# A perceiver block planned anew: measured overlaps, waits for buffers at first use, and one context buffer per batch

## The chip, the cores and the metric

The kernel runs on one core of a Trainium2 chip. The metric is the device time of one execution in microseconds (us), and 0.2% of it is 3.3 us. Five engines work side by side: TensorE (PE, with its weight loads as PEld), VectorE (DVE), ScalarE (ACT), GpSimd (POOL) and SyncE (SP), which only issues transfers. Each works through its own list of instructions in order, and waits for the others where data or buffers require it.

## The reference

One block with two layers on 32 batches of 64 latents, width 256, with 256 context rows per batch, all in float32. What the change touches is the first part, the cross attention, and the order of everything:

```
kv_in  = concat(norm(ctx)[256 rows], norm(x)[64 rows])   # per batch: 320 rows
q      = norm(x) Wq ;  k = kv_in Wk ;  v = kv_in Wv      # 16 heads of 64
x      = x + softmax(q k^T / 8) v Wo                     # cross attention
x      = x + linear_attention(norm(x))
x      = x + ffn(norm(x))                                # int weights, dequantised
x      = x + attention(norm(x), norm(ctx)), masked
x      = x + slstm(norm(x))
x      = x + experts(norm(x))        # routed by an entmax over the experts
```

## The kernel before

**Tiles and stages.** The 2048 latent rows are 16 tiles of 128 rows, so a tile t holds the batches 2t and 2t+1. The kernel has three stages. The first is the cross attention over 32 batches, about 0 to 854 us. The second runs linear attention, feed forward, attention, sLSTM and router in 8 groups of two tiles, to about 1390 us. The third runs the experts on gathered rows, to the end.

**The cross attention.** For a pair of batches, `l0_context` loads two contexts into one tile `cx` of 128x1024 (four row tiles of 256), norms the four row tiles, and applies gain and offset (`affine`) on GpSimd in instructions over the whole tile. Two such tiles fit (`ar.put(1, "cx", ...)`). `l0_keys` transposes a batch's context (`tr_c`) into `cT`. `l0_scores` has eight score matmul groups (`sc`, two heads each; first the four with even numbers, then the odd ones). Each has a maximum on DVE (`nmax`) and an exp on ACT, which also sums. After four of them come a reciprocal, a divide of 128x1280 on DVE and three stream transposes. When both halves are there, sixteen pieces are moved into `pT`: four on GpSimd, four on ACT or DVE, eight as transfers from SP. `l0_applied` multiplies with the normed context (`pu`): twice, two pairs of matmuls with 128 rows, and one pair with 64 rows for the latents' part. Each result is copied to `uT` on ACT or DVE. `l0_projected` projects a pair of batches: `po`, which reads the copies, and then `pw`. For every four batches `l0_queries` makes norms, transposes, `pq` and the eight products `pqk`, whose copies fill the buffers `qk`.

**Second and third stage.** Names beginning with `la` (`lakv`, `lakvs`, `lac`, `laq`) belong to linear attention, `ff` to feed forward, `xa`, `xsc`, `xpTp`, `xpo`, `xpw` to attention, `sl` to sLSTM, `me`, `lg` and `gT_ps` to the router, and `mepha`, `mepya`, `mephb`, `mepyb`, `rl`, `rg`, `tr_xg` to the experts. Names that begin with `tr_` are transpositions on TensorE.

**The order.** No instruction's place is written out by hand. The kernel first lists all operations with their operands and a rank (`pl.rank`), and then a planner (`Plan.run`) replays a model of the chip. Among the operations whose predecessors are placed and whose buffers have room, it takes the one that can start first, and among equals the one with the lower rank; it looks at most a fixed number of ranks ahead. It issues that operation at once, so the order in which it picks is the order of each engine's list. The planned times themselves are not kept: on the chip only data, buffers and the order count. The model has a length for each instruction (`PlanEngine.length`), one for each TensorE group (`together(length)`), and 0.06 us (`HOP`) from the end of one instruction to a dependent one on another engine. `copy` and `either` are operations that ACT or DVE can do; the planner chooses the engine that can start sooner. A tile takes a place in `Slots` or in an `Area` when its first operation is issued; the place comes free after the last one that uses it. Every instruction is recorded by the one line in `issue`, which is why all rows of the profile show L375. The core of the planner's choice:

```python
for engine, (length, _) in op.ways.items():
    at = free[engine]
    for other in op.before:
        at = max(at, other.end if other.on == engine and other.end == other.done else other.done + self.HOP)
    for t_ in op.uses:
        at = max(at, t_.free_at)
    key = at, op.rank
    if best is None or key < best[0]:
        best = key, op, engine
...
op.end = op.done = free[engine] = at + length
```

Of the kernel before, what the change touches and what calls it, by code (L numbers as in the profile page):

```python
# [8 lines left out]
F32 = mybir.dt.float32  # L9
# [5 lines left out]
P = 128  # L15
# [139 lines left out]
class Slots:  # L155
# [5 lines left out]
    def room(self, t_, k):  # L161
        return len(self.free) > k and (not self.in_order or self.asked[self.next + k] is t_)

    def take(self, t_):
        self.free.sort()
        self.next += 1
        return self.free.pop(0)
# [5 lines left out]
class Area:  # L173
# [9 lines left out]
    def room(self, t_, k):  # L183
        i = (self.next + k) % len(self.places)
        if k >= len(self.places) or self.asked[self.next + k] is not t_ or self.live[i] is not None:
            return False
        return all(a.next == len(a.asked) and a.live[j] is None for a, j in self.rivals[i])

    def take(self, t_):
        i = self.next % len(self.places)  # L190
# [19 lines left out]
class Plan:  # L210
# [8 lines left out]

    ENGINES = {"PE": "tensor", "DVE": "vector", "ACT": "scalar", "POOL": "gpsimd", "SP": "sync"}  # L220
    HOP = 0.06

    def __init__(self, tc):
        self.tc, self.ops, self.slots, self.news = tc, [], {}, []
# [25 lines left out]
    @contextmanager  # L250
    def together(self, length):

        assert self.group is None
        self.group = []
        yield
        calls, self.group = self.group, None
        self.add({"PE": (length, calls)})

    def add(self, ways):
        op = Op()  # L260
# [38 lines left out]
    def run(self, ahead):  # L299
        free = dict.fromkeys(self.ENGINES, 0.0)  # L300
        busy = dict.fromkeys(self.ENGINES, 0.0)
        wire = 0.0
        ready = [op for op in self.ops if op.left == 0]
        todo = len(self.ops)
        waiting = set(self.ops)
        rest = sorted(self.ops, key=lambda op: -op.rank)
        while todo:
            best, short = None, None
            while rest[-1] not in waiting:
                rest.pop()  # L310
            for op in sorted(ready, key=lambda op: op.rank):
                if short is not None and op.rank > short.rank and "PE" in op.ways and op.news:
                    continue
                if op.rank > rest[-1].rank + ahead:
                    continue
                at = 0.0
                if op.news and not self.has_room(op):
                    if "PE" in op.ways and (short is None or op.rank < short.rank) and self.has_room(op, True):
                        short = op
                    continue  # L320
                for engine, (length, _) in op.ways.items():
                    at = free[engine]
                    for other in op.before:
                        at = max(at, other.end if other.on == engine and other.end == other.done else other.done + self.HOP)
                    for t_ in op.uses:
                        at = max(at, t_.free_at)
                    key = at, op.rank
                    if best is None or key < best[0]:
                        best = key, op, engine
            assert best is not None, "nothing can start"  # L330
            (at, _), op, engine = best
            length, calls = op.ways[engine]
            todo -= 1
            ready.remove(op)
            waiting.remove(op)
            op.on = engine
            op.end = op.done = free[engine] = at + length
            busy[engine] += length
            if "dma" in calls[0][0]:
                size = PlanEngine.size_of(calls[0])  # L340
                wire = max(wire, op.end) + size / 380e3
                op.done = max(wire, op.end + size / 220e3) + (2.4 if engine == "POOL" else 1.5)
            self.issue(op, engine, calls)
            for other in op.after:
                other.left -= 1
                if other.left == 0:
                    ready.append(other)
        self.now, self.busy = max(op.done for op in self.ops), busy

    def has_room(self, op, later=False):  # L350

        taken = {}
        for t_ in op.news:
            s_ = t_.slots
            if later and not s_.in_order:
                continue
            k = taken.get(id(s_), 0)
            if not s_.room(t_, k):
                return False
            taken[id(s_)] = k + 1  # L360
        return True

    def issue(self, op, engine, calls):
        for t_ in op.news:
# [74 lines left out]
class PlanEngine:  # L439
# [33 lines left out]
    @staticmethod  # L473
    def length(engine, name, args, kw):

        if "dma" in name:
            return (0.65 if isinstance(kw["in_"], View) and isinstance(kw["out"], View) else 0.4) if "indirect" not in name else 1.55 if "compute_op" in kw else 1.25
        o = args[0] if args else kw["out"]
        n = 1
        for a in [o] + [a for a in args[1:] if isinstance(a, View)]:  # L480
            m = 1
            for k in a.shape[1:]:
                m *= k
            n = max(n, m)
        if name == "memset":
            return 0.1 + 0.5e-3 * n
        if engine == "ACT":
            if isinstance(kw.get("scale"), View):
                return 0.6
            return (0.12 + 0.91e-3 * n if name == "copy" else 0.33 + 0.66e-3 * n) + (0.19 if "accum_out" in kw else 0)  # L490
        if engine == "DVE":
            return 0.15 + 1.04e-3 * n + (0.08 if name == "tensor_tensor_reduce" else 0)
        if engine == "POOL":
            return 0.7 if n < 64 else 0.3 + 2.0e-3 * n
        return 0.18 if name == "transpose" else max(0.36, 1.67e-3 * n)


# [1 line left out]
def kernel(ctx: ExitStack, tc: tile.TileContext, d: dict, out: bass.AP):  # L499
# [130 lines left out]
    with ExitStack() as sa:  # L630
# [18 lines left out]
        ar.put(1, "gb", 1024, 10240)  # L649
        for n, tag in enumerate(("la", "ls", "latT")):  # L650
            ar.put(1, tag, 512, 11264 + 512 * n, 12800 + 512 * n)
        ar.put(1, "cx", 1024, 14336, 15360)
        ar.put(1, "cT", 640, 16384, 17024)
        ar.put(0, "gbcol", 256, 17664, 17920)
        ar.put(1, "qk", 1024, *range(17664, 25856, 1024))
# [118 lines left out]
        def l0_context(t):  # L774

            pl.rank = 2 * t - 6.0
            cx = ar.tile([P, 4, D], F32, tag="cx", name=f"cx{t}")
            for b2 in range(2):
                b = 2 * t + b2
                pl.sync.dma_start(  # L780
                    out=cx[:, 2 * b2 : 2 * b2 + 2, :],
                    in_=d["ctx"][b * S2 : (b + 1) * S2, :].rearrange("(t p) d -> p t d", p=P),
                )
            if t == 0:
                load_w(wv, "l0x_wkv", slice(1024, 2048))
                load_w(wo, "l0x_wo")
            if t == 2:

                nxt["a_wq"] = ar.tile([P, KD, D], F32, tag="a_wq", name="a_wq")
                pl.sync.dma_start(out=nxt["a_wq"], in_=d["a_wq"].rearrange("(k p) n -> p k n", p=P))  # L790
                nxt["a_wkv"] = ar.tile([P, KD, 2 * D], F32, tag="a_wkv", name="a_wkv")
                pl.sync.dma_start(out=nxt["a_wkv"], in_=d["a_wkv"].rearrange("(k p) n -> p k n", p=P))
                nxt["rows_a"] = ar.tile([P, 4 * D], F32, tag="rows_a", name="rows_a")
                pl.sync.dma_start(out=nxt["rows_a"], in_=d["rows"][:, 0 : 4 * D].to_broadcast([P, 4 * D]))
                pl.sync.dma_start(out=rows, in_=d["rows"][:, 4 * D :].to_broadcast([P, NROWS - 4 * D]))
            pl.rank = 2 * t - 3.0
            srcs = [cx[:, i, :] for i in range(4)]
            norm(srcs, srcs, f"c{t}", "c")
            affine(cx, 0, 4)
            return cx  # L800

        def l0_queries(g):
# [52 lines left out]
        def l0_keys(b, lt, cx):  # L855

            pl.rank, pl.lane = b - 1.2, "k"
            b2, b4 = b % 2, b % G
            cT = ar.tile([P, KD, SK], F32, tag="cT", name=f"cT{b}")
            pst = bank([P, KD, S2], f"tr_c{b}")  # L860
            with pl.together(T4):
                for kd in range(KD):
                    for i in range(2):
                        tr(pst[:, kd, i * P : (i + 1) * P], cx[:, 2 * b2 + i, kd * P : (kd + 1) * P], ident)
            pl.gpsimd.tensor_copy(cT[:, :, S2:SK], lt[:, :, b4 * S : (b4 + 1) * S])
            pl.copy(cT[:, :, 0:S2], pst)
            return cT
# [58 lines left out]
        def l0_applied(b, pT, cx, la, ls, uT):  # L926
# [5 lines left out]
            for kd in range(KD):  # L932
                f_ = slice(kd * P, (kd + 1) * P)
                pus = [bank([P, 4, 4, 32], f"pu{b}_{kd}_{jj}") for jj in range(2)]
                for jj in range(2):
                    with pl.together(1.75):
                        for n in range(2):
                            rhs = pT[:, 2 * n + jj].rearrange("p a j c -> p j a c")
                            mm(pus[jj], cx[:, 2 * b2 + n, f_], rhs, start=(n == 0), stop=False)
                with pl.together(1.04):  # L940
                    for jj in range(2):
                        h_ = slice(64 * jj, 64 * jj + 64)
# [991 lines left out]
```

## Time and profile before

| What | us |
|---|---|
| median of 3 runs (lowest, highest) | 1634.33 (1632.51, 1634.55) |
| profiled execution | 1633.02 |
| its span, first to last instruction | 1631.3 |
| first and last matmul in the span | 5.3, 1617.5 |

Of the costliest groups, some rows (engine, operation, tiles and shapes, count, then busy us and mean ns of one):

```profile
L375 PE MATMUL pu<-arena 128*128 128x512 f32 (+1 forms) x768 | 301.0, 615 | 3.5 <-ACT arena L375 2.8
L375 PE MATMUL sc<-arena 128*128 128x320 f32 x1024 | 290.5, 436 | 0.0
L375 ACT ACTIVATE arena<-sc,nmax 128x320 f32<-128x320 f32 x256 | 134.4, 527 | 250.3 <-DVE nmax L375 241.8
L375 DVE TENSOR_TENSOR arena<-arena,sm 128x1280 f32<-128x1280 f32 x64 | 108.1, 1690 | 2.2
```

The column after the last bar is the idle time of the engine just before these instructions, and what ended it. ACT waits long for DVE's maxima, but idle time of an engine that isn't the bottleneck costs nothing: TensorE's rows show next to none. On GpSimd by shape, the affine of the contexts and the same work in the second stage:

```profile
L375 POOL TENSOR_TENSOR arena<-arena 128x1024 f32<-128x1024 f32 x32 | 80.8, 2526 | 43.5 <-ACT arena L375 40.6 <-PE sc L375 1.7
...
L375 POOL TENSOR_TENSOR arena<-arena 128x512 f32<-128x512 f32 x16 | 21.6, 1351 | 22.4 <-DVE arena L375 12.1 <-ACT arena L375 9.6
```

### The profile page before, as it was taken

The numbers are of one execution on the slowest core, as the hardware profiler recorded it, in microseconds if no ns is written. First come the engines' busy times: TensorE is split into PE (matmuls) and PEld (weight loads), VectorE is DVE, ScalarE is ACT, GpSimd is POOL, SyncE is SP. The second block draws the span as 40 slices with busy tenths as digits, with TensorE's granted clock in tenths as the row PEclk, the third lists the DMA queues.
The fourth block names the chain that finished last, engine by engine and source line by source line (L and its number), as shares of the span: only waits on it lengthen the run. The fifth ranks groups of instructions, "written<-read, shape, count | busy, mean of one in ns | idle before, by whom it ended". The sixth has DMA issues, their size and how long they took to land. (4 is left out here: it accounts for less than half of the span.)

```text
span 1631.3 us, 25951 instructions
## 1 busy us (share of the span) xinstructions
PE 1579.4 (97%) x9226; PEld 1106.8 (68%) x9226; DVE 1088.2 (67%) x3089; ACT 693.8 (43%) x1813; POOL 422.1 (26%) x524
## 2 busy tenths in 40 slices
PE   8999999999999999999989999999999999999996
PEld 6556656565665656666556777777777776878885
DVE  6657666676766757776755788888888788762230
ACT  4434344353533535334421454454544547432332
POOL 5123123230333223331311221221212112223342
PEclk9999999999999999999999999999999999999998
DMA  6112112121112211122121000010000220455391
GB/s 212 38 30 59 38 31 44 38 59 29 39 30 46 47 34 40 30 71 53 38 54 49 14 27 27 18 37 14 27 27 20 85 80 19 133 144 141 69 307 31
DMA packets 95601, 95.02 MB, mean 58 GB/s; under 512 B 9327, under 2 KB 85936, under 8 KB 95472
## 3 DMA queue, kind: packets, MB, share of 16 engines
q1 hardware_dynamic: 89952, 85.41, 19.2%
q0 software_dynamic: 5520, 7.94, 2.4%
q8 instruction: 74, 1.21, 0.3%
q14 instruction: 55, 0.45, 0.1%
HBM read 63.63 MB, written 7.47 MB: 44 GB/s over the span
## 5 line engine op out<-in xcount | busy, mean ns | idle before, releaser
L375 PE MATMUL pu<-arena 128*128 128x512 f32 (+1 forms) x768 | 301.0, 615 | 3.5 <-ACT arena L375 2.8
L375 PE MATMUL sc<-arena 128*128 128x320 f32 x1024 | 290.5, 436 | 0.0
L375 PEld LDWEIGHTS sc<-arena 128*128 128x128 f32 x1024 | 190.8, 190 | 95.3 <-issue 19.2
L375 ACT ACTIVATE arena<-sc,nmax 128x320 f32<-128x320 f32 x256 | 134.4, 527 | 250.3 <-DVE nmax L375 241.8
L375 PEld LDWEIGHTS pu<-arena 128*128 128x128 f32 (+1 forms) x768 | 113.9, 189 | 175.9 <-issue 159.1
L375 POOL COPY arena<-arena 32x640 f32<-32x640 f32 (+1 forms) x161 | 108.9, 676 | 404.1 <-DVE arena L375 300.4
L375 DVE TENSOR_REDUCE nmax<-sc 128x1 f32<-128x320 f32 x256 | 121.8, 484 | 105.5 <-PE sc L375 104.1
L375 POOL TENSOR_TENSOR arena<-arena 128x1024 f32<-128x1024 f32 (+3 forms) x72 | 118.5, 1646 | 166.6 <-DVE arena L375 109.7
L375 ACT ACTIVATE arena<-arena,xnm 128x256 f32<-128x256 f32 x256 | 127.1, 500 | 52.1 <-DVE xnm L375 51.9
L375 DVE COPY arena<-pu 128x512 f32<-128x512 f32 x62 | 42.7, 689 | 115.4 <-PE pu L375 115.2
L375 DVE CUSTOM_DVE_ANT_0 arena<-xsc,arena 128x256 f32<-128x256 f32 x256 | 101.2, 421 | 17.7 <-ACT arena L375 10.3
L375 DVE TENSOR_TENSOR arena<-arena,sm 128x1280 f32<-128x1280 f32 x64 | 108.1, 1690 | 2.2
L375 DVE STREAM_TRANSPOSE arena<-arena 128x512 f32<-128x512 f32 (+1 forms) x192 | 104.4, 594 | 3.6
L375 ACT COPY arena<-pu 128x512 f32<-128x512 f32 x66 | 38.4, 585 | 128.0 <-PE pu L375 128.0
L375 POOL DMA_INDIRECT out<-arena x25 | 39.6, 1585 | 102.8 <-DVE arena L375 71.2
L375 PE MATMUL pqk<-arena 64*128 64x256 f32 x512 | 63.1, 383 | 1.6 <-ACT arena L375 1.6
L375 PE MATMUL xpTp<-ident,arena 128*128 128x128 f32 x512 | 63.6, 274 | 0.9 <-ACT arena L375 0.9
L375 PE MATMUL xak<-arena 128*128 128x512 f32 x128 | 62.3, 610 | 0.0
L375 PEld LDWEIGHTS xpTp<-ident,arena 128*128 128x128 f32 x512 | 56.9, 141 | 7.2 <-DVE arena L375 2.2
L375 PE MATMUL xav<-arena 128*128 128x256 f32 x256 | 61.5, 384 | 0.0
L375 PEld LDWEIGHTS po<-arena 128*64 128x64 f32 x1024 | 55.5, 137 | 8.8 <-issue 8.3
L375 PE MATMUL mepha<-arena 128*128 128x256 f32 x256 | 60.1, 385 | 1.4 <-ACT arena L375 1.4
(395 smaller groups left out, 2800.9 us busy)
## 6 DMA issues: line engine op xcount, KB each, us to landing
arena<-in_m_w SPq DMA_DIRECT2D x26, 1024.0 KB
arena<-arena SPq DMA_DIRECT2D x256, 80.0 KB
arena<-in_ctx SPq DMA_DIRECT2D x32, 256.0 KB
arena<-in_ctxT SPq DMA_DIRECT2D x16, 512.0 KB
x<-in_x SPq DMA_DIRECT2D x16, 128.0 KB
arena<-in_l0x_wkv SPq DMA_DIRECT2D x2, 1024.0 KB
arena<-arena SPq DMA_DIRECT2D x16, 128.0 KB
out<-x SPq DMA_DIRECT2D x16, 128.0 KB
```

The lines of the kernel that those rows point to most:

```text
L375: r = getattr(real, name)(*[get(a) for a in args], **{k: get(a) for k, a in kw.items()})
```

## The change

The planner's model gets five corrections, and one tile is cut in two.

- After an instruction, DVE is free for the next 0.085 us before its end, ACT 0.11, POOL 0.05.
- An operation that depends on one of the same engine can start 0.03 us after that one's end instead of at its end.
- TensorE groups are planned 1.5% shorter.
- An operation that takes a new buffer and itself uses it isn't planned before that buffer is free.
- Lengths of several instructions are changed: activations are at most 0.6 us, an accumulated sum adds 0.09 instead of 0.19, GpSimd's copies cost 0.15 + 0.97e-3 n, and others.
- A context is loaded into one tile of 128x512 for each batch, in four places instead of two of twice the size. The norm still goes over the pair, the affine over each batch: 64 instructions for 32.

```diff
+    def when(self, k):                       # Slots
+        return sorted(self.free)[k]
+    def when(self, k):                       # Area
+        i = (self.next + k) % len(self.places)
+        return max([self.last[i]] + [a.last[j] for a, j in self.rivals[i]])
...
     HOP = 0.06
+    OVERLAP = {"DVE": 0.085, "ACT": 0.11, "POOL": 0.05}
...
-        self.add({"PE": (length, calls)})
+        self.add({"PE": (0.985 * length, calls)})
...
+                since = self.since(op)
                 for engine, (length, _) in op.ways.items():
-                    at = free[engine]
+                    at = max(free[engine], since)
                     for other in op.before:
-                        at = max(at, other.end if other.on == engine and other.end == other.done else other.done + self.HOP)
+                        at = max(at, other.done + (0.03 if other.on == engine else self.HOP))
...
-            op.end = op.done = free[engine] = at + length
+            op.end = op.done = at + length
+            free[engine] = op.end - self.OVERLAP.get(engine, 0.0)
...
+    def since(self, op):
+        at, taken = 0.0, {}
+        for t_ in op.news:
+            k = taken.get(id(t_.slots), 0)
+            taken[id(t_.slots)] = k + 1
+            if t_ in op.uses:
+                at = max(at, t_.slots.when(k))
+        return at
...
-            return 0.1 + 0.5e-3 * n
+            return 0.12 + 0.5e-3 * n
...
-            return (0.12 + 0.91e-3 * n if name == "copy" else 0.33 + 0.66e-3 * n) + (0.19 if "accum_out" in kw else 0)
+            return (0.12 + 0.91e-3 * n if name == "copy" else min(0.33 + 0.66e-3 * n, 0.6)) + (0.09 if "accum_out" in kw else 0)
...
-            return 0.15 + 1.04e-3 * n + (0.08 if name == "tensor_tensor_reduce" else 0)
+            return 0.15 + 1.04e-3 * n + (0.02 if name == "tensor_tensor_reduce" else 0)
...
-            return 0.7 if n < 64 else 0.3 + 2.0e-3 * n
+            if n < 64:
+                return 0.7 if n <= 2 else 1.0
+            return 0.15 + 0.97e-3 * n if name == "tensor_copy" else 0.3 + 1.9e-3 * n
...
-        ar.put(1, "cx", 1024, 14336, 15360)
+        ar.put(1, "cx", 512, *range(14336, 16384, 512))
...
-            cx = ar.tile([P, 4, D], F32, tag="cx", name=f"cx{t}")
+            cx = [ar.tile([P, 2, D], F32, tag="cx", name=f"cx{t}_{b2}") for b2 in range(2)]
...
-            affine(cx, 0, 4)
+            for b2 in range(2):
+                affine(cx[b2], 0, 2)
```

`l0_keys` and `l0_applied` read `cx[b2]` instead of a half of `cx`. The arithmetic is the same.

More of the change, by code (lines that the diff above doesn't have):

```diff
@@ L780, in l0_context @@
                 pl.sync.dma_start(
-                    out=cx[:, 2 * b2 : 2 * b2 + 2, :],
-                    in_=d["ctx"][b * S2 : (b + 1) * S2, :].rearrange("(t p) d -> p t d", p=P),
+                    out=cx[b2], in_=d["ctx"][b * S2 : (b + 1) * S2, :].rearrange("(t p) d -> p t d", p=P)
                 )
@@ L796, in l0_context @@
             pl.rank = 2 * t - 3.0
-            srcs = [cx[:, i, :] for i in range(4)]
+            srcs = [cx[i // 2][:, i % 2, :] for i in range(4)]
             norm(srcs, srcs, f"c{t}", "c")
-            affine(cx, 0, 4)
+            for b2 in range(2):
+                affine(cx[b2], 0, 2)
             return cx
@@ L863, in l0_keys @@
                     for i in range(2):
-                        tr(pst[:, kd, i * P : (i + 1) * P], cx[:, 2 * b2 + i, kd * P : (kd + 1) * P], ident)
+                        tr(pst[:, kd, i * P : (i + 1) * P], cx[b2][:, i, kd * P : (kd + 1) * P], ident)
             pl.gpsimd.tensor_copy(cT[:, :, S2:SK], lt[:, :, b4 * S : (b4 + 1) * S])
@@ L938, in l0_applied @@
                             rhs = pT[:, 2 * n + jj].rearrange("p a j c -> p j a c")
-                            mm(pus[jj], cx[:, 2 * b2 + n, f_], rhs, start=(n == 0), stop=False)
+                            mm(pus[jj], cx[b2][:, n, f_], rhs, start=(n == 0), stop=False)
                 with pl.together(1.04):
```

## The prediction

> **What bounds the kernel now.** I read first the busy shares and the forty slices, then who the matrix engine waits for, then its own timeline at each of those waits, and last the busy time in single stretches.
>
> ```profile
> PE 1579.4 (97%) x9226; PEld 1106.8 (68%) x9226; DVE 1088.2 (67%) x3089; ACT 693.8 (43%) x1813; POOL 422.1 (26%) x524
> PE   8999999999999999999989999999999999999996
> ```
>
> TensorE is busy 97% of the span in every slice but the first, one in the middle and the last. Its gaps add up to 38.2 us, beside a tail of 13.8 us after its last matmul. A new order can win only from these gaps, from clock lost after them and from dearer transitions between matmuls; it can lose without limit by putting a matmul before its data. The waits of TensorE (total, times, longest):
>
> ```profile
> PE lakvs L375 <- DVE arena L375: 5.3, 1, 5.3
> ...
> PE pu L375 <- ACT arena L375: 2.8, 1, 2.8
> PE gT_psB L375 <- DVE arena L375: 2.4, 1, 2.4
> ...
> PE pqk L375 <- ACT arena L375: 1.6, 7, 0.2
> ...
> PE pu L375 <- DVE arena L375: 0.6, 3, 0.2
> ```
>
> Three single waits are large; the rest are small ones that recur. The stretches (us, then busy of PE, weight load, DVE, ACT, POOL, clock, DMA share, GB/s):
>
> ```profile
> 79.60:83.00 3.40, 3.38 (x5) 1.61 (x6) 3.33 (x6) 0.00 (x0) 0.00 (x0) 0.57 0.00 0
> 574.00:615.00 41.00, 41.00 (x187) 24.08 (x187) 24.74 (x45) 15.01 (x40) 5.29 (x7) 1.00 0.13 30
> 850.50:854.00 3.50, 3.37 (x24) 2.75 (x25) 2.54 (x12) 0.00 (x0) 0.15 (x2) 0.51 0.61 115
> 1189.00:1230.00 41.00, 40.43 (x322) 29.30 (x313) 33.83 (x130) 18.90 (x55) 7.88 (x13) 1.00 0.08 27
> ```
>
> Row 2 is the steady cross attention: no gap in 41 us. Row 4 is the second stage: 0.57 us lost in 41. Rows 1 and 3 are two stretches just after a wait, at little over half the clock. So in the cross attention the present order can hardly be bettered, and each new wait adds its whole length.
>
> **The change, part by part.** Sums are against the profiled execution, 1633.0 us (span 1631.3). I compared the two orders engine by engine: the same matmuls, 82% of them between the same neighbours; 23 copies and activations go from DVE to ACT; POOL has 32 instructions more.
>
> *Buffers and affine.* POOL's 32 instructions on 128x1024 (mean 2.53 us) become 64 on 128x512; the row of that shape in the second stage has 1.35. That is 64 × 1.35 − 32 × 2.53 = +5.4 us for POOL, which is idle 1209 us, and each context is normalised about a batch (25 us) before its use: nothing on the path. Without that cover it would be 16 × 0.35 us. A load can start one batch sooner, but its place in SP's queue is nearly unchanged, and DMA is 13% busy there: nothing.
>
> *Cross attention, projection.* Before, one or two score groups stood between a batch's last `pu` and `po`, which reads copies of that `pu` (ACT 0.585, DVE 0.689 us). Now the scores stand before the last 64-row `pu` pair; `po` follows directly on 6 even pairs (2 to 12), and behind a `tr_c` (0.44 us) on 7 odd ones. The trace has one bare case, `po0` (TensorE's timeline: start, us, group, wait before it):
>
> ```profile
> 90.42 0.44 PE L375 MATMUL po<-arena 128*64 128x128 f32 x4
> 91.16 1.75 PE L375 MATMUL po<-arena 128*64 128x128 f32 x28 [0.30 <-ACT arena L375]
> ```
>
> Here the gap is 0.30, and the lost time against an undisturbed group 0.62 us. With `tr_c` in front 0.62 − 0.44 = 0.18. So 6 × 0.62 + 7 × 0.18 = **+5.0** (between +2 and +8: copies queued behind other work would be later still).
>
> *Cross attention, `pu` and `pqk`.* The shortest cover between a batch's last score and the `pu` that reads its weights rises from 11.9 to 14.7 us. The chain between them (reduce, exp, divide, transposes, moves) takes 11.3 in the one case where nothing else runs, batch 31. The waits at `pu5`, `pu9`, `pu13` (0.35 each) go: **−1.1**. `pqk_7` loses 1.02 us seven times because its banks wait for copies on ACT behind exps. Those exps now come later, but so do the copies' followers; I take less than half, 7 × 0.45 = **−3.1** (0 to −7). The wait at `pu1` (2.77) is shortened by two score groups of about 0.9 less what they displace: **−1.1** (to −2.6 if the slow clock behind it, 1.5 us, goes too).
>
> *Transitions.* A `pu` matmul on 128 rows starts 0.429 us after one on 128, the first on 64 rows 0.522 us after; score to `pu` 0.269, score to `po` 0.362. Each change of row layout thus costs 0.093. I count 409 such changes in the old order and 396 in the new: **−1.2**.
>
> *From cross attention to second stage.* The old order, last score to last `pu`, on the same timeline:
>
> ```profile
> 842.70 1.88 PE L375 MATMUL lakv<-arena 128*128 128x512 f32 x4
> 844.51 0.71 PE L375 MATMUL lakvs<-arena 64*128 64x129 f32 x8
> 850.54 1.23 PE L375 MATMUL lakvs<-arena 64*128 64x129 f32 x8 [5.32 <-DVE arena L375]
> 851.70 2.21 PE L375 MATMUL lac<-arena 128*64 128x136 f32 x16
> 854.03 9.42 PE L375 MATMUL pu<-arena 128*128 128x512 f32 x24
> ```
>
> `sc31_7` ends at 842.70, `pu31` starts at 854.03: a chain of 11.33 us, beside which 4.1 us of matmuls (at full clock) run; 7.2 are lost. The new order does the first `lakv` and half of the `lakvs` earlier, and has one `pu30` pair (1.1), `lakvs` (0.65) and `lac` (1.1) there: 2.83 us. Two `pu30` copies come into the queues of the chain, half of one (0.35) on its path. Lost: 11.33 + 0.35 − 2.83 = 8.85, or +1.65. The wait is now in two parts: the copies of `lakvs` stand on DVE behind batch 31's divide, transposes and moves, so `lac0_1` waits some 4.4 us and `pu31` some 4. `tr_ff0` (0.7 lost) gets `po15` in front: −0.7.
>
> Here a rule speaks against the change. The Trainium skill ("TensorE: Matmul & The Clock Gate", Part 1: The HAM clock gate) says that the clock halves after about 3.4 us of idleness and needs about 3.4 us of activity to recover. By it one stall costs 1.7 us extra, the two together 3.4, and shorter waits nothing. The rows say: 0.51 for 3.5 us after 5.32 idle, but 0.57 for 3.4 us after only 2.77. So the row makes even short waits dear; the second stall follows closely and shares part of the slow time, so I take +1 for the second (0 to 1.7). Sum **+2**, 0 to +4.
>
> *Second stage.* Eight groups of 67.4 us, each losing 2.2 us. The new order tightens links: cover from the first `xsc` half to its transposes 4.25 us (5.3 before), while in group 5 the seventh exp ends 4.0 us after `xsc`; `tr_sl` after `xpw` 3.46 (5.2), against about 3.5 for the chain through the addition, norm and copy, added up from its rows; `lg` has one 0.55 us group after `tr_me` instead of an `xsc`. `tr_me` itself gains 0.7 of cover and its 0.3 wait goes. About +0.25 a group: **+2**, from −7 (half of the 2.2 goes) to +16 (rival 3).
>
> *Hand-over to the experts.* Between the router's `lg7` and `gT_psB` the order had 8.4 us of matmuls and a wait of 2.37; now 7.35: wait about 3.5, +1.1. `gT_psA` has 9.4 instead of 10.3 and a wait of 0.65: +0.9. `xpTp13` has 6.1 us behind its scores instead of 10: +1. **+3**, between −5 and +6, as 10 us are lost between 1299 and 1394 already. Experts and tail: one gather and its transposition come earlier, and on SP two small loads change places with their neighbours; all are asked for long before their use: **0** (−2 to +4).
>
> Sum: 5.0 − 1.1 − 3.1 − 1.1 − 1.2 + 2 + 2 + 3 = +5.5, or 1638.5 profiled. The median of the three runs (1634.3) lies 1.3 above the profiled execution, so **1639.8**.
>
> **Rivals.** A kernel of this spread (1632.51 to 1634.55) tells 0.2%, 3.3 us, from no change.
>
> 1. *Faster: the measured lengths put DVE and ACT work where it fits.* `pqk` −5, `pu` −1.1, `pu1` −1.1, transitions −1.2, `po` only +3.5, boundary +1, second stage −5: −8.9, or **1625.4**. For it: ACT is 43% busy, and every recurring wait of before is on ACT or DVE. It wins once the second stage gains 0.6 us a group. Against it: the covers above shrink more often than they grow. 0.25.
> 2. *No change.* TensorE is full, and what the links lose elsewhere is refilled: without the +5 of second stage and hand-over, **1634.8**. 0.18.
> 3. *The second stage's links run dry in each group.* The three covers that equal their chains within 0.3 us all fall short, and a late link delays the next: +2 us in each of 8 groups, 1633 + 3.5 + 16 + 1.3 = about **1654**. It decides from a shortfall of 0.5 us at two links. Against: a late link leaves slack to the next. 0.17.
>
> That the change does not do what it says is excluded for the buffers (the order shows 64 halves); whether the planned overlaps are the chip's is rival 3's question.
>
> The forecast has 0.40: its own range is 1637 to 1646. The range for 8 in 10 cuts into rivals 1 and 3: 1625 to 1653. Faster 0.25; same 0.18; slower 0.40 + 0.17 = 0.57.
>
> **What would show it.** Some 13 new short waits of `po` on ACT or DVE, 0.2 to 0.6 us; no waits of `pu5`, `pu9`, `pu13`; fewer of `pqk`; waits of `lac` and `pu` near 845 to 856, with a clock of 0.5 to 0.6 behind them; `gT_psB` at 3.5; POOL rows 128x512 at 1.35 us, 80 of them. If the steady cross attention still has 41.0 of 41 busy, my +5 is wrong; if 67.4 us a group becomes 66.8 or 69.4, rival 1 or 3 holds.

## The result: 1.4% slower, and the profile after

The changed kernel takes 1655.85 us (median of 4 runs, 1654.69 to 1657.79) against 1633.87 (4 runs) before: ratio 1.0137, 95% interval 1.0119 to 1.0154. Its profiled execution has a span of 1653.6 us against 1631.3. Forecast were 1639.8 us and a range up to 1653.0: the direction was right, the size was not, and the time lies outside the range. One execution of adds_later (below), at 2216.9 us and a granted clock of 0.68 instead of 0.99, is left out of its median and its ratio.

From the page of the changed kernel, the busy shares and TensorE's forty slices:

```profile
PE 1574.9 (95%) x9226; PEld 1101.5 (67%) x9226; DVE 1047.6 (63%) x3066; ACT 699.6 (42%) x1836; POOL 433.8 (26%) x556
...
PE   7999999999999999999989999999999998999996
```

TensorE is busy 4.5 us less than before in a span that is 22.3 us longer; so some 27 us more of idle time. Its largest waits after the change (us in total, times, longest):

```profile
PE laq L395 <- ACT arena L395: 9.4, 6, 1.7
PE lac L395 <- DVE arena L395: 5.3, 1, 5.3
PE gbp L395 <- DVE tok L632: 5.3, 1, 5.3
PE tr_lat L395 <- POOL arena L395: 3.4, 5, 0.7
PE tr_la L395 <- DVE arena L395: 3.2, 5, 0.7
PE pu L395 <- DMA arena<-arena: 2.9, 1, 2.9
PE xrT L395 <- DVE r_xa L395: 2.8, 6, 0.5
PE ffg L395 <- DVE arena L395: 2.8, 5, 0.6
```

Before, the list was led by single waits, `gbp` ahead of the first matmul (5.3, as now) and the three that the prediction shows. Now `laq`, `tr_la`, `xrT` and `ffg`, all in the second stage, wait five or six times each. One period of that stage (from one group's `lg` to the next one's), first before and then in the changed kernel; the columns are us, then busy of PE, weight load, DVE, ACT, POOL, clock, DMA share, GB/s:

```profile
1064.30:1131.73 67.43, 66.44 (x517) 49.61 (x513) 55.29 (x199) 33.70 (x98) 13.36 (x25) 1.00 0.08 25
```

```profile
1072.72:1142.46 69.74, 66.03 (x512) 48.94 (x512) 53.47 (x198) 34.34 (x100) 13.24 (x25) 1.00 0.07 24
```

Of the 69.74 us TensorE stands 3.7, of the 67.4 before 1.0. Laid beside the trace of before, the changed kernel is late by 3.5 us at the last `pw` but two (`pw13`, end of the steady cross attention), 6.1 at `lg0`, 15.4 at `lg4`, 23.5 at the first `mephb` (which lies inside the experts), 22.3 at the end.

These differences can't be read as they stand, because the new order puts work behind `lg` that the old one does before it. TensorE at the first `lg` of the changed kernel:

```profile
1002.97 1.06 PE L395 MATMUL lg<-arena 128*128 128x8 f32 x8
1003.89 1.96 PE L395 MATMUL xak<-arena 128*128 128x512 f32 x4
1005.69 1.89 PE L395 MATMUL ffu<-arena 128*128 128x256 f32 x8
1007.51 1.15 PE L395 MATMUL xsc<-arena 32*128 32x256 f32 x16
```

Before, such groups of `xak`, `ffu` and `xsc` start at 991.28, 993.10 and 995.83 us, ahead of `lg` at 996.90. Counted by tiles, up to `pw13` and up to the first `mephb` both kernels have done the same matmuls; at `lg0` and at `lg4` the changed one has these 28 still to do, 4.7 us (1003.89 to 1008.58). With them, the cross attention costs 3.5 us, the stretch from `pw13` to `lg0` 7.3 (2.6 and the 4.7), the four groups to `lg4` 9.3, the stretch from there to `mephb` 3.4 (8.1 less the 4.7), and the experts give back 1.2. `laq` waits its 1.72 in five groups: the four, and the one just before `lg0`. So five late groups, at 2.33 each, make 11.7 us, and the passage between the stages without its late group 5.0.

What a late group looks like, on TensorE's timeline (start, us, group, wait before it):

```profile
1033.75 1.99 PE L395 MATMUL xaq<-arena 128*128 128x256 f32 x8
1036.40 0.82 PE L395 MATMUL tr_la<-ident,arena 128*128 128x128 f32 x4 [0.65 <-DVE arena L395]
1037.06 1.88 PE L395 MATMUL xak<-arena 128*128 128x512 f32 x4
1040.66 1.99 PE L395 MATMUL laq<-arena 128*128 128x256 f32 x8 [1.72 <-ACT arena L395]
```

The same place before:

```profile
1030.87 0.55 PE L375 MATMUL tr_la<-ident,arena 128*128 128x128 f32 x3 [0.37 <-ACT arena L375]
1031.35 1.61 PE L375 MATMUL xsc<-arena 32*128 32x256 f32 x16
1032.89 1.99 PE L375 MATMUL ffg<-arena 128*128 128x256 f32 x8
1034.72 1.89 PE L375 MATMUL laq<-arena 128*128 128x256 f32 x8
```

The old order had an `xsc` and an `ffg` between `tr_la` and `laq`, 3.4 us of work; the new one has one `xak`, 1.8 us. What VectorE and GpSimd did just before, from their own timelines of the changed kernel:

```profile
1031.60 0.73 DVE L395 TENSOR_TENSOR t_lay<-r_lay,ve_lay 128x2 f32<-128x2 f32 x1
1032.36 0.65 DVE L395 SCALAR_TENSOR_TENSOR t_lay<-t_lay,r_lay 128x2 f32<-128x2 f32 x1
1033.04 0.16 DVE L395 SCALAR_TENSOR_TENSOR r_lay<-t_lay,r_lay 128x2 f32<-128x2 f32 x1
1033.12 0.15 DVE L395 TENSOR_TENSOR t_la<-r_la,ve_la 128x2 f32<-128x2 f32 x1
```

```profile
1030.91 0.69 POOL L395 TENSOR_TENSOR r_la<-ve_la,mhalf 128x2 f32<-128x2 f32 x1
1031.58 1.42 POOL L395 TENSOR_TENSOR x<-x,rows 128x256 f32<-128x256 f32 x2
```

Two steps on two numbers per partition take 0.73 and 0.65 us beside two GpSimd additions of 0.7 each, and each ends when one of these does; as soon as the additions are over, such a step takes 0.15. `t_la` leads to `tr_la`. The Trainium skill ("SBUF — State Buffer", SBUF: two separate sides) has the rule: VectorE instructions with two SBUF inputs and GpSimd instructions that read SBUF share a port pair as an exclusive lock, and "the other fully blocks" for the whole instruction. The planner doesn't know of it. By the plan's 0.15 the two steps together would have taken 0.3 us; by the rows they took 1.4. Steps with one SBUF input are held too: `ve_c` on 128x4 takes 0.46 us (mean of 14) beside a GpSimd copy, almost always one of 32x640, and 0.17 alone.

Summed over the 29 small norm steps of one group, what each takes over 0.16 us comes to 2.3 us in the changed kernel and to 0.6 before.

### The profile page after: what moved, and what is told of

Read it like the earlier page. It is cut to its first block, busy times and chain, and to the rows that moved or that the text cites. A ratio compares the mean times of both kernels' runs of the same rounds, so it can differ in the third digit from the quotient of the medians.

```text
span 1653.6 us, 25992 instructions
## 1 busy us (share of the span) xinstructions
PE 1574.9 (95%) x9226; PEld 1101.5 (67%) x9226; DVE 1047.6 (63%) x3066; ACT 699.6 (42%) x1836; POOL 433.8 (26%) x556
## 5 line engine op out<-in xcount | busy, mean ns | idle before, releaser
L395 PE MATMUL pu<-arena 128*128 128x512 f32 (+1 forms) x768 | 305.5, 616 | 4.5 <-DMA arena<-arena 2.9
L395 PE MATMUL sc<-arena 128*128 128x320 f32 x1024 | 294.5, 436 | 2.4 <-DVE arena L395 2.4
L395 PEld LDWEIGHTS sc<-arena 128*128 128x128 f32 x1024 | 194.3, 191 | 103.7 <-issue 33.4
L395 POOL COPY arena<-arena 32x640 f32<-32x640 f32 (+1 forms) x161 | 123.5, 767 | 434.4 <-DVE arena L395 388.1
L395 POOL TENSOR_TENSOR arena<-arena 128x512 f32<-128x512 f32 (+2 forms) x104 | 118.7, 1161 | 125.8 <-DVE arena L395 101.7
L395 DVE TENSOR_TENSOR arena<-arena,sm 128x1280 f32<-128x1280 f32 x64 | 101.3, 1582 | 1.9
L395 POOL TENSOR_TENSOR arena<-xsm,arena 128x256 f32<-128x256 f32 x32 | 20.4, 637 | 192.0 <-DVE xsm L395 118.4
L395 PE MATMUL po<-arena 128*64 128x128 f32 x1024 | 61.3, 275 | 2.7 <-DVE arena L395 2.4
```

The costliest lines, as they stand in the source:

```text
L395: r = getattr(real, name)(*[get(a) for a in args], **{k: get(a) for k, a in kw.items()})
```

## The experiments

Ratios are against the kernel before on the same chip. Its median was 1633.9 us for the changed kernel, 1631.8 to 1632.2 for the runs to lock_pez, and 1628.1 for the last four; so the expectations in us, which start from 1655.9, are better compared by ratio. "Late at" compares single profiles with the one of before (from the first chip), in us. Four orders that are the same up to `pw0` reach it up to 2.2 us apart, so differences along a row say more than the last column. The columns `lg0` and `lg4` are too low by the work moved behind `lg`: 4.7 us in the changed kernel, planner_alone, la_first, adds_later, la_adds and pe_zero; about 2.9 (`ffu` and `xsc`) in old_lengths and the runs from lock to lock_pez_q; nothing in cx_alone and lock_old_planner.

| run | median us | ratio, 95% | late at `pw13` | `lg0` | `lg4` | `mephb` | end |
|---|---|---|---|---|---|---|---|
| changed | 1655.9 | 1.0137 (1.0119 to 1.0154) | 3.5 | 6.1 | 15.4 | 23.5 | 22.3 |
| cx_alone | 1641.0 | 1.0052 (1.0040 to 1.0064) | 3.9 | 8.9 | 8.9 | 8.3 | 6.4 |
| planner_alone | 1648.7 | 1.0101 (1.0068 to 1.0135) | 1.3 | 3.2 | 12.5 | 16.8 | 13.3 |
| la_first | 1653.6 | 1.0119 (1.0088 to 1.0150) | 1.3 | 6.5 | 15.6 | 23.6 | 21.8 |
| adds_later | 1644.4 | 1.0075 (1.0048 to 1.0102) | 2.9 | 3.0 | 4.9 | 12.3 | 11.4 |
| la_adds | 1643.0 | 1.0081 (1.0064 to 1.0098) | 1.9 | 1.7 | 3.3 | 10.6 | 8.5 |
| pe_zero | 1646.2 | 1.0093 (1.0076 to 1.0110) | −6.0 | −2.5 | 6.9 | 14.9 | 12.9 |
| lock | 1635.3 | 1.0024 (1.0012 to 1.0036) | 0.5 | 1.5 | 5.1 | 7.4 | 5.9 |
| lock_pez | 1628.9 | 0.9979 (0.9969 to 0.9989) | −6.2 | −5.3 | −1.4 | −2.7 | −4.1 |
| lock_pez_31 | 1616.2 | 0.9927 (0.9910 to 0.9943) | −3.4 | −12.9 | −9.3 | −10.5 | −16.4 |
| lock_pez_q | 1612.2 | 0.9899 (0.9883 to 0.9916) | −6.2 | −16.9 | −17.6 | −14.4 | −17.4 |
| lock_old_planner | 1645.0 | 1.0102 (1.0085 to 1.0119) | 5.5 | 12.4 | 15.5 | 18.1 | 12.6 |
| old_lengths | 1646.0 | 1.0116 (1.0098 to 1.0133) | 1.3 | 7.7 | 14.6 | 17.4 | 11.5 |

**cx_alone** has the change's edits of `cx` and `affine`, and no other.

> Only the context buffers and the affine per batch are changed; the planner is that of before. Theory A (the loss comes from the planner's order in the second stage): no change, 1632 to 1636 us, because 99% of TensorE's order stays. Rival B (twice as many GpSimd instructions hold up the transposition of the latents, 0.7 us five times in the changed kernel): 1636 to 1638.

Both missed: 0.5% slower. The second stage keeps 67.4 us a group, and `tr_lat` doesn't wait five times. But one `tr_lat` at the start waits 4.0 us for GpSimd, and at the end of the cross attention the order differs: `lakv` and `lakvs` come earlier, and `lac` then waits 5.28 and `pu31` 3.01, as in the changed kernel (5.0 us between `pw13` and `lg0`, with the same matmuls there as before). 99% of an order being the same says nothing of the other 1%.

**planner_alone** is the changed kernel with the context in one tile of 128x1024.

> All five corrections of the planner, with the context in one tile for two batches as before. Theory A: the whole loss stays, 1652 to 1658. Rival B (the buffers and the affine's halves carry part): 1648 to 1652, with the waits of the latents' transposition gone.

A group takes 69.74 us as in the changed kernel, so the second stage's loss is the planner's. The median lies in rival B's range and the interval is wide (by the ratio 1645 to 1656), but the waits of `tr_lat` (0.68) are still there, so the halves of the affine didn't cause them. `lac` and `pu31` wait here too (5.45 and 1.99): either half of the change alone brings the two waits of the passage. The two parts (0.52% and 1.01%) add up to the whole within their intervals.

**la_first** replays the changed kernel's order, with one ACT instruction moved in five groups:

```diff
+        for e in [e for e in line if e[0].mark == "la" and e[1] == "ACT"]:
+            i = line.index(e)
+            act = [k for k in range(i) if line[k][1] == "ACT"][-3:]
+            to = [k for k in act if line[k][0].mark == "xaq"]
+            if to and all(line.index(b) < to[0] for b in line if b[0] in e[0].before):
+                line.insert(to[0], line.pop(i))
```

> The changed kernel's order is replayed, with one instruction moved in five groups of the second stage: ACT's copy of tr_la stands one place earlier, before the activation that reads xaq. Theory A1 (that activation waits for two VectorE instructions that the plan did not count on, and the copy behind it makes laq late): the wait of laq, 1.72 in five groups, falls to about 0.2, so 1655.9 - 7.5 = 1648, between 1646 and 1650. Rival A2 (the copy is late because tr_la and all of VectorE are late; another wait takes its place at the next link): less than 2 us of gain, 1654 to 1657.

`laq` no longer waits in these groups, and a group is no shorter (69.7 us). The waits of this kernel, from the same view:

```profile
PE tr_ff L416 <- ACT arena L416: 4.5, 6, 0.8
...
PE xpTp L416 <- ACT arena L416: 3.2, 7, 0.6
```

`tr_ff` waits 0.8 and `xpTp` 0.5 in each group instead: 1.3 of the 1.72 come back at once. A2 holds: the copy's place isn't what makes a group late.

**adds_later** replays the same order, with GpSimd's additions of `beta` and `x_bo` moved back behind `r_ff` and the next product:

```diff
+        for e in [e for e in line if e[0].mark == "add"][::-1]:
+            i = line.index(e)
+            last = min([k for k in range(i, len(line)) if e[0] in line[k][0].before], default=len(line))
+            at = e[0].end + 13.0
+            to = next(k for k in range(i + 1, len(line)) if line[k][0].end > at)
+            line.insert(min(to, last) - 1, line.pop(i))
```

> The changed kernel's order is replayed, with GpSimd's additions of the beta and x_bo rows in the second stage (two and two in a group) placed about 13 us later, behind their group's small norm steps. Theory C (VectorE's steps on 128x2 take 0.5 to 0.7 us instead of 0.15 beside these additions, and this delays tr_la, xaq and laq): those steps fall to about 0.15, the wait of tr_la (0.65) goes and that of laq falls by about 1, so 1655.9 - 6 x 1.6 = about 1646, between 1644 and 1649. Rival A1 alone (it is the copy's place in the queue that counts): only tr_la's wait is moved on to laq, 1653 to 1656.

Theory C holds, with 1644.4. No other engine's order was touched; the steps on 128x2, first in the changed kernel, then here (VectorE groups by shape: count, busy us, mean ns):

```profile
L395 DVE TENSOR_TENSOR t_ff<-r_ff,ve_ff 128x2 f32<-128x2 f32 x8 | 4.5, 561 | 0.3 <-POOL r_ff L395 0.2
...
L395 DVE TENSOR_TENSOR t_lay<-r_lay,ve_lay 128x2 f32<-128x2 f32 x8 | 4.3, 538 | 0.5 <-POOL r_lay L395 0.5
L395 DVE SCALAR_TENSOR_TENSOR t_lay<-t_lay,r_lay 128x2 f32<-128x2 f32 x8 | 4.2, 528 | 0.3
```

```profile
L416 DVE TENSOR_TENSOR t_ff<-r_ff,ve_ff 128x2 f32<-128x2 f32 x8 | 1.4, 169 | 0.3 <-POOL r_ff L416 0.2
...
L416 DVE SCALAR_TENSOR_TENSOR t_lay<-t_lay,r_lay 128x2 f32<-128x2 f32 x8 | 1.3, 161 | 0.3
...
L416 DVE TENSOR_TENSOR t_lay<-r_lay,ve_lay 128x2 f32<-128x2 f32 x8 | 1.2, 153 | 0.5 <-POOL r_lay L416 0.5
```

The wait of `tr_la` is gone, that of `laq` is 0.9 instead of 1.72, and a group takes 67.88 us: 1.86 of the 2.33 us. Summed as above, the norm steps of a group take 0.5 us over 0.16 each, instead of 2.3.

**la_adds** makes both moves.

> Both moves at once in the changed kernel's order: GpSimd's additions 13 us later, and ACT's copy of tr_la before the activation that reads xaq. With the additions moved alone a group took 67.9 us with 0.9 left at laq. Theory C (lock first, place second): laq's wait goes and little takes its place, 67.0 to 67.3 a group, 3 to 4.5 us faster than with the additions moved alone. Rival A2 (as with the copy moved alone, the next links tr_ff and xpTp take it over): within 1.5 us of the additions alone.

The rival holds: 67.82 a group, and the ratios of the two runs overlap. `laq`'s 0.9 turns up as 0.3 at `tr_ff` and 0.5 at `xpTp`.

**pe_zero** is the changed kernel with

```diff
-                        at = max(at, other.done + (0.03 if other.on == engine else self.HOP))
+                        at = max(at, other.done + ((0.0 if engine == "PE" else 0.03) if other.on == engine else self.HOP))
```

> The changed kernel, planned without the 0.03 us between dependent TensorE groups (VectorE, ScalarE and GpSimd keep it). The order then has scores behind the last pu pair again before each po. Theory D (that 0.03 us is what let score groups into the middle of a pu, and po then waits for bare copies): the waits of po (six of 0.4, 0.6 us lost each) go, the second stage stays at 69.7 us a group: 3 to 5 us faster than the changed kernel. Rival (po's waits come from the lengths or the overlap): unchanged within 1.5 us.

Theory D holds and was too modest. No `po` waits; the five waits of `tr_lat` (0.8 lost each) and those at `pqk` go as well, and one new wait of 1.8 at a `tr_lat` comes. Against the changed kernel it gains 9.5 us up to `pw13`, and a group still takes 69.7, with the norm steps as slow as there. With 0.03 us on each dependent TensorE group, the second pair of a `pu` could start 0.03 later than any independent group; the planner takes what starts first. In TensorE's timeline of the changed kernel four scores stand inside each `pu` of the steady part, ahead of its 64-row pair; in pe_zero's none does.

**lock** adds to the changed kernel's planner what the trace shows:

```diff
                     at = max(free[engine], since)
+                    if PlanEngine.locks(engine, calls_):
+                        at = max(at, held["POOL" if engine == "DVE" else "DVE"])
...
+            if PlanEngine.locks(engine, calls):
+                held[engine] = op.end
...
+    def locks(engine, calls):   # GpSimd tensor work; VectorE with two tensors, none in PSUM
+        name, args, kw = calls[0]
+        if engine == "POOL":
+            return "tensor" in name
+        return engine == "DVE" and name in ("tensor_tensor", "scalar_tensor_tensor") and not any(
+            isinstance(a, View) and a.tile.psum for a in args)
```

> The changed kernel, with one more rule in the planner: a GpSimd tensor instruction and a VectorE instruction with two SBUF operands are not planned at the same time. Theory C: the plan then has the delays that the chip has, the VectorE steps before tr_la are ordered clear of the additions, and a group of the second stage falls to about 67.4 us or less: 1640 to 1648. Rival (any new order of this planner brings its own late links, since it fills every gap to the last 0.1 us): 1650 or more.

The time, 1635.3, is below theory C's range, but not in the way it said: `t_lay` is at 0.16 us and the norm steps of a group take 0.4 us over 0.16 each, yet a group is at 68.3 and not 67.4, because `tr_la` waits 1.36 and `slp` 1.05. The stretch from `lg4` to `mephb` costs 2.3 us instead of 8.1, without the moved work nothing instead of 3.4. This plan differs from the changed kernel's on all engines, so it agrees with adds_later but isolates less.

**lock_pez** has the lock rule and pe_zero's edit.

> The lock rule and no 0.03 us on TensorE together. If the two causes are separate, their gains add up: the gain of the lock rule alone plus 3 to 5 us. If this comes under 1632 it beats both kernels.

The gains add up, and pe_zero's part is above the 3 to 5 us expected: lock is 1.1% and pe_zero 0.4% below the changed kernel, this one 1.6%. It is 0.2% faster than the kernel before.

**lock_pez_31** gives batch 31 an earlier rank:

```diff
-                    pl.rank = b - 1.6 + 0.1 * (4 * jj + jp)
+                    pl.rank = b - 1.6 + 0.1 * (4 * jj + jp) - (0.5 if b == 31 else 0.0)
```

> The lock rule, no 0.03 us on TensorE, and the last batch's scores ranked 0.5 lower: sc31_5 and sc31_7 stand before pu30 instead of behind it. Theory E (the 7.7 us of waits between the stages are the chain of 11.3 us from the last score to pu31, with nothing put beside it): pu30's 9.4 us now cover it, the waits of lac and pu31 fall under 1 us and the slow clock behind them goes: 6 to 9 us faster than without the edit, 1620 to 1623. Rival (pu30 then waits for its own weights, because the two scores were its cover): at most 3 us faster.

TensorE's timeline between the stages in lock_pez, and then in this kernel:

```profile
835.44 2.42 PE L400 MATMUL sc<-arena 128*128 128x320 f32 x8
837.79 1.16 PE L400 MATMUL lakvs<-arena 64*128 64x129 f32 x16
839.19 0.42 PE L400 MATMUL lac<-arena 128*64 128x136 f32 x2 [0.24 <-ACT arena L400]
841.16 0.68 PE L400 MATMUL lac<-arena 128*64 128x136 f32 x6 [1.55 <-DVE arena L400]
845.12 1.49 PE L400 MATMUL lac<-arena 128*64 128x136 f32 x8 [3.28 <-DVE arena L400]
849.51 11.56 PE L400 MATMUL pu<-arena 128*128 128x512 f32 x24 [2.90 <-DMA arena<-arena]
```

```profile
833.69 6.77 PE L400 MATMUL pu<-arena 128*128 128x512 f32 x18
840.29 1.06 PE L400 MATMUL lakvs<-arena 64*128 64x129 f32 x16
841.89 1.82 PE L400 MATMUL lac<-arena 128*64 128x136 f32 x16 [0.54 <-DVE arena L400]
843.72 9.42 PE L400 MATMUL pu<-arena 128*128 128x512 f32 x24
```

Waits of 8 us become 0.5, and `pu` takes 9.42 us instead of 11.56: in lock_pez the granted clock is 0.50 from 843.6 to 853.8, while here it is 1.00 through the whole `pu`. Between `pw13` and `lg0` that is 10.5 us, and 0.5% by the ratios. Theory E holds.

**lock_pez_q** is lock_pez_31 and

```diff
+        if op.mark == "xaq" and self.ops and self.ops[-1].mark == "xaq":
+            op.before.add(self.ops[-1])
```

> The lock rule and no 0.03 us on TensorE as before, and two more edits: the scores of the last batch get a rank 0.5 lower, so that all eight stand before pu30, and each of the four instructions that read xaq is planned after the one before it, as the built program makes them wait. Theory: as in the run with the first edit alone, and tr_la's wait of 1.36 us in five groups shrinks by half: 2 to 4 us faster than that run. Rival (as the copy's move showed: another link takes it): within 1.5 us of it.

The theory holds: `tr_la` waits 0.60 instead of 1.36, a group takes 67.24 us, and the median is 4.0 us lower. At 0.9899 (0.9883 to 0.9916) this version beats the kernel before by 1.0% and the changed one by 2.4%. Why is open. In lock_pez_31, as in the changed kernel, the four readers of `xaq` are VectorE, VectorE, ACT, VectorE, and one begins only when the one on the other engine has ended (2.2 us in all; before, they alternate and take 2.3). The Trainium skill ("PSUM — Partial Sum Buffer", PSUM bank collisions raise a hardware error) says that the compiler makes accesses of two engines to one bank and quadrant depend on each other, reads too; they also write interleaved halves of one tile, and no run here tells these two apart. With the edit the planner gives all four readers to VectorE, where they take 2.5 us. So the gain doesn't come from faster readers, and knowing the dependence isn't separated from the new place of the work.

**lock_old_planner** has the buffers of the change, the old planner and the lock rule.

> One context buffer per batch, the planner of before without its five corrections, and the lock rule alone. Theory C (the lock matters where a plan is tight enough to put norm steps beside additions, which the corrections made it): little gain over the buffers alone (1641), 1637 to 1641. Rival (the lock rule is worth its 20 us under any plan): under 1630.

The rival falls, and the theory was too kind: it is slower than cx_alone (1.0102 against 1.0052). A group takes 67.7 to 69.4 us, with two waits of 0.48 for the readers of `xaq`. A true rule added to a plan gives another order, not surely a better one.

**old_lengths** is the changed kernel with the old `PlanEngine.length`.

> The changed kernel with the old lengths of instructions, the other four corrections kept. The order then has 3.5 us of matmuls more between tr_la and laq. Theory (the lengths led to the short cover, the lock does the rest): laq's wait of 1.72 goes, tr_la's stays, 67.5 to 68.5 a group, 1641 to 1649. Rival (the lock's delay is there under any lengths and shows at the next link): 1651 or more.

The rival is nearer. `laq` no longer waits, but `tr_ff` does (0.69) and `slp` (1.49), and a group takes 69.1 us, more than the theory allows. The 1646.0 us lie in the theory's range only because the chip is faster: the ratio 1.0116 is 1652.8 us against the 1633.9 of the first one, in the rival's range. The norm steps show more: they take 0.9 us over 0.16 each in a group, with the new lengths 2.3. So most of the collisions came with the lengths, and a group can be late by 1.7 us with few of them.

## Why the prediction was wrong

**Second stage: the step that failed.** "About +0.25 a group: **+2**" measured +2.33 a group in five groups, +11.7; that is 9.7 of the 16.8 us between the forecast's +5.5 and the 22.3 measured. The covers named there (`xpTp`, `tr_sl`, `lg`) didn't run dry. `tr_la`, `laq`, `xrT` and `ffg` did, and they weren't among the links looked at, although the order showed that `laq` had come nearer to `tr_la`. The deeper error: chain lengths were taken from the trace of before, as if a step kept its length. What stands beside a step is part of what an order changes, and the price was in that trace:

```profile
L375 DVE TENSOR_TENSOR t_sl<-r_sl,ve_sl 128x2 f32<-128x2 f32 x8 | 3.7, 468 | 4.0 <-POOL r_sl L375 3.9
...
L375 DVE TENSOR_TENSOR t_lay<-r_lay,ve_lay 128x2 f32<-128x2 f32 x8 | 1.2, 153 | 0.4 <-POOL r_lay L375 0.3
```

The same step takes 0.153 us in `t_lay`, and in `t_sl`, where a GpSimd instruction on 128x256 stands beside it, up to 0.57. The new order frees `t_sl` and puts `t_lay` and `t_ff` beside the additions. adds_later shows that these collisions are 1.86 of the 2.33 us in this order. Rival 3 had nearly the right time, 1654, and nearly the right size for a group, but named links that held: that is luck.

**Hand-over.** Forecast were +3 and a share of the second stage; from `lg4` to `mephb`, with three more groups, 3.4 is measured without the moved work. The sum was right, partly by luck. `gT_psA` waits 1.32 as worked out. The wait of 3.5 forecast at `gT_psB` came one step sooner and smaller, as 2.31 at `tr_me` in the same chain, but with 6.8 us at half clock behind it, where `gT_psB`'s 2.37 had 3.4 before.

**Buffers and affine.** Costed at nothing "on the path". GpSimd's instructions are as forecast (80 on 128x512, 1.31 us each) and hidden in the steady part, but the change alone costs 0.52%: with the new places the planner orders the start and the passage between the stages differently.

**Cross attention, projection.** +5.0 was right where it was worked from a row: six waits of 0.41, 0.63 us lost each. On the odd pairs, behind a `tr_c`, no `po` waited. The five waits of `tr_lat`, 0.8 us lost each, were overlooked. The stretch from 574 to 615 us now has 40.72 us busy, not 41.00.

**`pu` and `pqk`.** The waits at `pu5`, `pu9` and `pu13` went. The last two `pqk` of a group lose 0.78 us together instead of 1.02: seven times 0.24 is 1.7 gained, not 3.1. The wait at `pu1` is 1.58 instead of 2.77 and its slow clock went too, more than the 1.1 forecast; but a new wait of 2.0 at a `sc` has its own 3.4 us at half clock behind it, at 33.3 us, and at `pw0` the two kernels are level. From there to `pw13` the terms with a row make 3.8 (`po`) + 4.0 (`tr_lat`) − 1.7 − 1.1 = +5.0, and +3.5 is measured, for a forecast of −1.5. The forecast's transitions (−1.2) would fit the rest, but the gain can't be separated in these runs: by the number of rows alone the traces have 278 changes before and 279 after.

**Between the stages.** Two waits, 5.3 at `lac0_1` and 2.9 at `pu31`: 8.2 us for 8.85 forecast. In all the passage cost 5.0 for +2. These two waits were right in size and the wait of `tr_ff0` went as forecast, but the next `tr_ff` waits 2.04, which was not looked at. The clock behind them in the changed kernel, in the same columns as above:

```profile
851.00:854.50 3.50, 0.09 (x1) 0.12 (x2) 3.41 (x7) 1.45 (x2) 2.35 (x3) 0.72 0.25 47
854.50:858.70 4.20, 1.39 (x8) 0.90 (x8) 3.63 (x17) 0.00 (x0) 2.17 (x4) 0.50 0.62 117
858.70:862.20 3.50, 3.41 (x4) 1.51 (x5) 2.87 (x17) 0.00 (x0) 1.55 (x2) 0.50 0.02 5
```

The second stall falls into the slow time of the first and prolongs it: the clock is at half for 10.2 us here and for 6.8 before, but TensorE stands in part of it, so a share and not the whole of a second slow window was right.

**What bounds the kernel.** Two readings there were loose, and change no term: a 9 in the forty slices means 90% or more, while 97% is the mean of the whole span; and the 38.2 us of gaps include 5.3 ahead of the first matmul.

**What was shown.** By one engine's order alone: GpSimd's additions beside the norm's steps cost 1.86 us a group (adds_later). By one edit of the planner, which changes the whole order: the 0.03 us on TensorE (pe_zero), the last batch's scores (lock_pez_31), and in agreement with adds_later the lock (lock). Left open: 0.47 us of a group's 2.33, what makes `tr_la` and `slp` wait under the lock rule, and how much the other corrections add; old_lengths shows only that most collisions came with the lengths.

## What to carry to other kernels

When an order changes, don't carry over durations from the old trace: look at what each step will stand beside, and at VectorE and GpSimd work on SBUF first of all. A planner with finer times fills every gap, so what it leaves out (here a lock) or puts in wrongly (here a cost between dependent matmuls) decided more than the tenths that were corrected. Before laying two traces beside each other at a landmark, count what each has done up to it: here 4.7 us of matmuls had changed sides. And moving the instruction that a matmul waits for only moves the wait, unless the chain in front of it gets shorter.

## What the runs showed of the hardware

A VectorE step on 128x2 takes 0.15 us alone and up to 0.73 beside a GpSimd addition on 128x256: nearly five times as long, for one of the smallest instructions in the kernel. In the traces of the two kernels waits of TensorE of 2.3, 2.4 and 2.8 us are followed by 3.4 to 6.8 us at a granted clock of 0.50, one of 1.6 is not, and of two waits of 2.0 after the change one is (at 31.7 us) and one is not (at 914.5). And executions whose order is the same up to there differ by up to 2.2 us at the first `pw`.
